# A graph-network layer on one core: 24 source columns a step on VectorE and on ScalarE, and six rows a step fetched by SyncE

## The chip, the core and the metric

The kernel runs on one core of a Trainium2 chip. The core has TensorE (PE in the profile; PEld is its weight loads), VectorE (DVE), ScalarE (ACT), GpSimd (POOL) and SyncE (SP), and 16 DMA engines that all of them share. Each engine works off its own list of instructions in order. An engine's list also holds instructions that its sequencer carries out itself (reading numbers into registers, computing an address, waiting for a semaphore, issuing a DMA); the profile does not count these as busy time of the engine.

The metric is the device time of one execution in microseconds (us), as the median of three runs. The profile is one further execution, with a time of its own.

## The reference

One layer of a graph network with residual and layer norm. There are 12,500 nodes of 64 features and 212,500 edges, sorted by the node they go to:

```python
msg_in = concat([nodes[row], nodes[col], edge_features], -1)
messages = relu(msg_in @ mW1 + mb1) @ mW2 + mb2
aggregated = segment_sum(messages, col, num_segments=12500)
upd_in = concat([nodes, aggregated], -1)
x = layernorm(x + relu(upd_in @ uW1 + ub1) @ uW2 + ub2)
```

`row` is the source of an edge and random; `col` is its destination, and rises along the list. All of it is in 32-bit floats.

## The kernel before

**Groups and steps.** The edges are cut into 554 groups of 384 (three tiles of 128). The loop in lines 718 to 777 makes one step for each group. In step `k` TensorE does three things one behind the other, with a single wait ahead of them and a single signal after the last (`step`, line 677): it transposes the gathered sources of group `k` (`turn`, line 423), multiplies group `k-2` by the message weights (`hidden`, line 448), and sums group `k-4` over destinations (`sums`, line 474). When the step has ended, ScalarE copies the transposed sources out of PSUM (line 440) and applies ReLU (line 464), and VectorE adds the sums into the aggregate (line 495) and the counts (line 496). TensorE's next step does not wait for these; the one after it does. The last ten groups (`SHORT`) take the three parts in a different order.

**Where the sources come from.** A group's 384 source rows reach the chip in one of two ways. Most groups are gathered by GpSimd: `gather` (line 181) issues one indirect DMA for each tile of 128 rows, 16 groups ahead (`AHEAD`), into a ring of 20 buffers. Every tenth or eleventh group is "columned" (`COPIED`): all nodes lie transposed in SBUF in `own.xc`, and VectorE and ScalarE copy one column of 64 floats for each edge from there to the group's place in `own.st` (`fetch`, line 585). Such a group needs no gather. `COLS` columns are copied in a step; `VCOLS` and `ACOLS` say how many by which engine and in which parts. Before, VectorE copies 12 and then 8 in a step, and ScalarE 16.

**Registers.** A column's address is read from a list in SBUF into a register. `registers(k, part)` (line 565) reads the addresses of one part with one instruction, TENSOR_LOAD (line 578), which the engine's sequencer carries out. `fetch(part)` then hands out that part's copies. Before, VectorE's part of 12 is loaded ahead of the additions (the list `between`, lines 493 and 738), its part of 8 just ahead of its copies, and ScalarE's part of 16 at the end of the step before (line 771). A further TENSOR_LOAD on VectorE, every fourth step, reads four registers that place the sums (`places`, line 366).

**SyncE.** For each step it issues the load of a 32-row window of projected nodes (`window`, line 390), every fourth step a block of edge features (`inputs`, line 355) into one of `BLOCKS` buffers, and every eighth step a list of column addresses (`indexes`, line 552). A window waits for TensorE to be done with the buffer.

**An unused path.** `STREAMS` describes single rows that an engine's queue can fetch by plain DMAs: the last tile of some groups (`BY_ROWS`) is then filled row by row (`row_numbers`, `row_fetch`, lines 632 and 652) into a buffer `own_side`, and not gathered. Before, the list is empty.

The destinations rise, so finished nodes can be updated while later groups are still worked on: every 22 steps or so `update` (line 500) runs the second network and the layer norm over 512 nodes, in pieces spread over several steps.

Of the kernel before, what the change touches and what calls it, by code (L numbers as in the profile page):

```python
# [32 lines left out]
G = (E + GE - 1) // GE  # L33
SB = 4
AHEAD = 16
RING = AHEAD + 4
BLOCKS = 4
NW = 2 * SB
COUNT = 96
NH = 3  # L40
# [9 lines left out]
TIMES = 4  # L50
BEGIN = 18
CHECKED = 8
VCOLS = (12, 8)
ACOLS = (16,)
COLS = sum(VCOLS + ACOLS)
SPAN = 8
STREAMS = ()
ROW_TURNS = 8
ROW_LEAD = 3

# [1 line left out]
def tiles_of(g):  # L62

    n = min(GE, E - g * GE)
    return [min(P, n - j * P) for j in range((n + P - 1) // P)]
# [26 lines left out]
BY_ROWS = []  # L92
for _, rate, _ in STREAMS:
    BY_ROWS.append([])
    while True:
        last = BEGIN + (P * (len(BY_ROWS[-1]) + 1) - 1) // rate + ROW_LEAD
# [7 lines left out]
class Own:  # L104
# [4 lines left out]
    def __init__(self, nc, ctx):  # L109
        def on(name, *shape, of=nc.sbuf_tensor):  # L110
            return ctx.enter_context(of(name, list(shape), F32)).ap()

        self.s = [on(f"own_s{i}", P, TG, D + W) for i in range(RING)]
        self.st = [on(f"own_st{i}", P, SB * GE) for i in range(BLOCKS)]
        self.wm = [on(f"own_wm{i}", P, H) for i in range(NW)]
        self.h = [on(f"own_h{i}", P, TG, H) for i in range(NH)]
        self.side = [[on(f"own_side{n}{i}", P, D + W) for i in range(2)]
                     for n in range(len(STREAMS))]
        self.ident = on("own_ident", P, P)
# [10 lines left out]
def ordered(ctx: ExitStack, tc: tile.TileContext, a, own, ok):  # L130
# [28 lines left out]
    def after(first, *others):  # L159

        tc.declare_no_dep(first.ins, group="quiet", reason="waits for the last of a step")
        for i in others:
            tc.add_manual_dep(
                first.ins, i.ins.name,
                mybir.DependencyInfo(mybir.DependencyClass.Sync, mybir.DependencyReason.DATA),
                reason="the kernel's own rings",
            )
        return first
# [73 lines left out]
    def bit(k):  # L242

        nodes = [NEAR_NODES + (N - NEAR_NODES) * i // BITS for i in (k, k + 1)]
        tiles = [first + (NT - first) * i // BITS for i in (k, k + 1)]
        nc.sync.dma_start(src_sb[:, slice(*tiles)], a["src"][:, slice(*tiles)])
        nc.sync.dma_start(xc[:D, slice(*nodes)], a["xT"][:, slice(*nodes)])
        rest(nodes[0], nodes[1] if k < BITS - 1 else NP)

    def zeroed(k):  # L250

        n0, n1 = (NP * i // BITS for i in (k, k + 1))
        nc.vector.memset(agg[:, n0:n1], 0.0)
# [58 lines left out]
    rows_by, row_index = {}, {}  # L312
    fetched = [[] for _ in STREAMS]
    issuers = {"SP": (nc.sync, ET.SP), "PE": (nc.tensor, ET.PE)}
# [40 lines left out]
    def inputs(b):  # L355
        if b * SB >= G:
            return
        c0, c1 = b * SB * GE, min(E, (b + 1) * SB * GE)
        efs_by[b] = nc.sync.dma_start(own.st[b % BLOCKS][D + W :, : c1 - c0], a["efT"][:, c0:c1])
        after(efs_by[b], *([hidden_by[(b - BLOCKS + 1) * SB - 1]] if b >= BLOCKS else []))  # L360

    def columns(g):
        t, c = own.st[g // SB % BLOCKS], (g % SB) * GE
        return t, c, sum(tiles_of(g))
# [58 lines left out]
    def turn(g, ps):  # L423
# [11 lines left out]
        def copy(step):  # L435
# [4 lines left out]
                after(nc.scalar.activation(t[r, c : c + n], xt[r, :n], AF.Copy), step))]  # L440
            if g >= BLOCKS * SB:
                after(copies[0], hidden_by[g - BLOCKS * SB])
            copy_by[g] = copies
# [30 lines left out]
    def sums(g, ps):  # L474
        h, s = own.h[g % NH], own.s[g % RING]
        sizes = tiles_of(g)
        sg = ps[2][:, : TIMES * W].rearrange("p (t w) -> p t w", w=W)
        counted = ps[2][0:1, TIMES * W :][:, :W]
        did = []
        for j, p in enumerate(sizes):  # L480
            did.append(nc.tensor.matmul(  # L481
                sg, h[:p, j, :],
                s[:p, j, D:].unsqueeze(1).to_broadcast([p, TIMES, W]),
                start=j == 0, stop=j == len(sizes) - 1))
        for j, p in enumerate(sizes):
            did.append(nc.tensor.matmul(counted, own.one[:p], s[:p, j, D:],  # L486
                                        start=j == 0, stop=j == len(sizes) - 1))

        def add(step):
            sums_by[g] = step  # L490
            at = bass.ds(starts.pop(g), W)
            count = xc[COUNT : COUNT + 1, at]
            if between:
                between.pop()()
            a = after(nc.vector.tensor_tensor(agg[:, at], sg[:, 0, :], agg[:, at], ALU.add), step)  # L495
            return [a, after(nc.vector.tensor_tensor(count, counted, count, ALU.add), step)]  # L496

        return did, [*relu_by[g], *copy_by[g]], add
# [66 lines left out]
    def registers(k, *parts):  # L565

        i, n = divmod(k - BEGIN, SPAN)
        if i < 0:
            return
        all_parts = [*((ET.DVE, c) for c in VCOLS), *((ET.Activation, c) for c in ACOLS)]  # L570
        for part in parts:
            engine, count = all_parts[part]
            c0 = (k - BEGIN) * COLS + sum(c for _, c in all_parts[:part])
            count = min(count, GE * len(COPIED) - c0)
            if count <= 0:
                return
            b = c0 - i * SPAN * COLS
            _, v = nc.values_load_multi_w_load_instructions(
                indices[i][0:1, b : b + count], engines=[engine],
                min_val=own.at, max_val=own.at + 4 * (N - 1),  # L580
                skip_runtime_bounds_check_because="a source is one of the nodes",
            )
            held[part] = engine, c0, v
# [28 lines left out]
    def row_span(n, i):  # L612

        _, rate, steps = STREAMS[n]
        size = ROW_TURNS * rate * steps
# [16 lines left out]
    def row_numbers(n, k):  # L632

        _, rate, steps = STREAMS[n]
        q, r = divmod(k - BEGIN, steps)
# [4 lines left out]
        if some > 0:  # L640
            _, v = nc.values_load_multi_w_load_instructions(
                row_index[n, i][0:1, b : b + some], engines=[issuers[STREAMS[n][0]][1]],
                min_val=0, max_val=4 * D * (N - 1),
# [69 lines left out]
    for n in range(len(STREAMS)):  # L713
        row_indexes(n, 0)
    made = summed = 0
    between, held, last = [], {}, {}

    for k in range(G):
        if k < BITS:
            bit(k)  # L720
            if k + 2 < BITS:
                zeroed(k + 2)
        if 1 < k < len(TABLE):
            projected(k)
        if k == CHECKED:
            addresses(0)
            for n in range(len(STREAMS)):
                row_addresses(n, 0)
            combined()
            ordered_edges()  # L730
            early.close()
            up = ctx.enter_context(tc.tile_pool(name="upd", bufs=2))
        if k % SB == 2:
            inputs(k // SB + 2)
        if k % SB == 1:
            places(k // SB + 1)
        if k < G - SHORT:
            between.append(lambda: registers(k, 0))
            step((turn, k), *([(hidden, k - 2)] if k > 1 else []),
                 *([(sums, k - 4)] if k > 3 else []))  # L740
            made, summed = max(0, k - 1), max(0, k - 3)
            if between:
                between.pop()()
        else:

            step((turn, k))
            for _ in range(2):
                if summed < made:
                    step((sums, summed))
                    summed += 1  # L750
            for _ in range(2):
                if made <= k:
                    step((hidden, made))
                    made += 1
            registers(k, 0)
        fetch(0)
        window(k + SB)
        for n in range(len(STREAMS)):
            row_numbers(n, k)
            row_fetch(n)  # L760
        onehot(k + LEAD)
        marks_by[k] = [copy_by[k][-1]]
        if k < G - 1:
            for part in range(1, len(VCOLS + ACOLS)):
                if part != len(VCOLS):
                    registers(k, part)
                fetch(part)
                if part >= len(VCOLS) and ET.Activation in last:
                    marks_by[k].append(last[ET.Activation])
            if k + 1 < G - 1:  # L770
                registers(k + 1, len(VCOLS))
            if k >= BEGIN and (k - BEGIN) % SPAN == 0:
                indexes((k - BEGIN) // SPAN + 1)
            if k >= BEGIN and (k - BEGIN) % SPAN == SPAN - 2:
                addresses((k - BEGIN) // SPAN + 1)
        if k + AHEAD < G:
            gather(k + AHEAD)
# [333 lines left out]
```

## Time and profile before

| what | value |
|---|---|
| median of three runs | 1914.63 us (1913.1 to 1914.86) |
| the profiled execution's own time | 1914.16 us |
| its span, first to last instruction | 1912.4 us |
| granted TensorE clock, mean | 0.972 |
| indirect gathers on POOL | 1514 |
| column copies on DVE and ACT | 10460 and 8356 |
| busy share of the span: POOL, PE, ACT, DVE | 75%, 69%, 69%, 65% |

A group row of the page names the line, the engine, the operation and the tiles, then the count, the busy time in us, the mean duration of one in ns, and the idle time of the engine just ahead of these instructions with what ended it. In a timeline row the first number is the start in us, the second how long the merged instructions took, and a bracket gives the idle time ahead and its releaser. "DVEq" and "ACTq" are those engines' sequencers, and a row of theirs gives the shortest, median and longest duration in ns.

### The profile page before, as it was taken

The page shows a single profiled execution, that of the slowest core. Times are in us where ns is not written, and L with a number is a line of the kernel's source. Part 1 is how long each engine was busy: PE and PEld are TensorE (multiplying, and loading weights), DVE is VectorE, ACT ScalarE, POOL GpSimd, SP SyncE. Part 2 cuts the span into 40 slices and gives each one's busy share as a digit, 9 for nine tenths or more (in the row PEclk, how much of TensorE's full clock was granted, in tenths as well). Part 3 has the DMA queues.
Part 4 walks back from the last instruction along what each step waited for, and adds up shares of the span by engine and source line. Part 5 has one row for each costly group of instructions (what it writes and reads, how often), then busy time and mean ns, then how long its engine had stood idle before and what let it go on. Part 6 is the DMA issues. An engine that isn't in the chain of part 4 may idle for free. (4 is left out here: it accounts for less than half of the span.)

```text
span 1912.4 us, 56586 instructions
## 1 busy us (share of the span) xinstructions
PE 1324.3 (69%) x12323; PEld 1170.6 (61%) x12323; DVE 1251.4 (65%) x12584; ACT 1325.2 (69%) x9559; POOL 1431.7 (75%) x1521
## 2 busy tenths in 40 slices
PE   5877777767767766676666776766766766667677
PEld 4766666666656655665655665655656655556566
DVE  4347777766666666676766766666667666676662
ACT  4468787766767767776767776776676677676662
POOL 7777777777777777777777777777777777777774
PEclk9889999989999999999999999999999999999998
DMA  5532222222222222222222212222222222222221
GB/s 141 139 97 64 53 50 52 49 49 48 45 53 52 46 52 48 49 49 48 53 48 48 50 44 53 52 46 52 48 50 48 51 47 52 45 53 48 49 50 25
DMA packets 113836, 105.15 MB, mean 55 GB/s; under 512 B 52115, under 2 KB 83488, under 8 KB 113488
## 3 DMA queue, kind: packets, MB, share of 16 engines
q0 software_dynamic: 48448, 49.68, 13.6%
q1 hardware_dynamic: 64196, 51.29, 9.7%
q8 instruction: 104, 1.70, 0.4%
q14 instruction: 244, 2.00, 0.3%
q10 hardware_dynamic: 844, 0.48, 0.1%
HBM read 91.68 MB, written 9.62 MB: 53 GB/s over the span
## 5 line engine op out<-in xcount | busy, mean ns | idle before, releaser
L184 POOL DMA_INDIRECT own_s<-in_x,src_sb x1514 | 1430.9, 945 | 462.5 <-issue 261.5
L599 DVE COPY own_st<-own_xc 64x4 uint8 x10460 | 896.5, 191 | 27.7 <-DMA by_dst<-t 3.5
L601 ACT ACTIVATE own_st<-own_xc 64x4 uint8 x8356 | 847.3, 195 | 2.9 <-DMA by_dst<-t 2.9
L429 PE MATMUL own_ps<-own_ident,own_s 128*96 128x128 f32 x1661 | 289.0, 284 | 540.4 <-DMA own_s<-in_x,src_sb 355.6
L440 ACT ACTIVATE own_st<-own_ps 96x384 f32<-96x384 f32 (+1 forms) x554 | 268.6, 485 | 506.7 <-PE own_ps L486 483.7
L429 PEld LDWEIGHTS own_ps<-own_ident,own_s 128*96 128x96 f32 x1661 | 164.3, 129 | 602.0 <-ACT own_h L464 445.0
L481 PE MATMUL own_ps<-own_s,own_h 128*128 128x128 f32 x3322 | 478.6, 282 | 1.3 <-ACT own_h L464 0.6
L495 DVE TENSOR_TENSOR own_agg<-own_ps,own_agg 128x32 f32 x554 | 106.3, 192 | 567.1 <-PE own_ps L486 386.4
L453 PE MATMUL own_ps<-own_wm,own_st 128*128 128x128 f32 x3322 | 476.5, 281 | 0.0
L481 PEld LDWEIGHTS own_ps<-own_s,own_h 128*128 128x128 f32 x3322 | 431.1, 198 | 2.8 <-ACT own_h L464 1.6
L453 PEld LDWEIGHTS own_ps<-own_wm,own_st 128*128 128x128 f32 x3322 | 428.6, 197 | 1.3 <-issue 0.5
L464 ACT ACTIVATE own_h<-own_ps 128x384 f32<-128x384 f32 x553 | 264.8, 479 | 21.2 <-PE own_ps L453 20.0
L486 PE MATMUL own_ps<-own_s,own_one 128*1 128x32 f32 x3322 | 189.1, 194 | 0.0
L486 PEld LDWEIGHTS own_ps<-own_s,own_one 128*1 128x1 f32 x3322 | 113.8, 83 | 69.4 <-issue 5.7
L412 DVE TENSOR_TENSOR own_s<-iota,dlc 128x96 f32<-128x96 f32 x554 | 137.3, 248 | 0.7
L496 DVE TENSOR_TENSOR own_xc<-own_ps,own_xc 1x32 f32 x554 | 102.1, 184 | 31.9 <-PE u_ps L507 13.2
L383 PE MATMUL u_ps<-w1b,own_xc 65*128 65x128 f32 x196 | 31.8, 310 | 32.0 <-DMA own_xc<-in_xT 12.7
L383 PEld LDWEIGHTS u_ps<-w1b,own_xc 65*128 65x128 f32 x196 | 26.8, 211 | 35.0 <-issue 20.3
L519 PE MATMUL u_ps<-same,own_xc 65*128 65x64 f32 (+1 forms) x196 | 39.5, 283 | 0.4 <-ACT u L512 0.4
L386 ACT ACTIVATE t<-u_ps 128x512 f32<-128x512 f32 (+1 forms) x25 | 14.7, 588 | 36.2 <-DMA by_dst<-t 20.0
L521 PE MATMUL u_ps<-u,u 128*128 128x64 f32 (+1 forms) x196 | 38.2, 277 | 0.0
L519 PEld LDWEIGHTS u_ps<-same,own_xc 65*128 65x128 f32 (+1 forms) x196 | 29.9, 192 | 2.5 <-ACT u L512 1.0
(60 smaller groups left out, 264.4 us busy)
## 6 DMA issues: line engine op xcount, KB each, us to landing
own_st<-in_efT SPq DMA_DIRECT2D x138, 192.0 KB
own_s<-in_x,src_sb POOLq DMA_INDIRECT x1514
own_wm<-by_dst SPq DMA_DIRECT2D x554, 16.0 KB
by_dst<-t SPq DMA_DIRECT2D x24, 256.0 KB
out<-o SPq DMA_DIRECT2D x24, 128.0 KB
own_xc<-in_xT SPq DMA_DIRECT2D x12, 179.2 KB
index<-in_src_copied SPq DMA_DIRECT2D x65, 1.1 KB
dlc_i<-in_dst_cols SPq DMA_DIRECT2D x1, 807.0 KB
```

The costliest lines, as they stand in the source:

```text
L184: nc.gpsimd.indirect_dma_start(out=s[:p, j, :D], out_offset=None, in_=x[:, :], in_offset=bass.IndirectOffsetOnAxis(ap=src_sb[:p, g * TG + ...
L412: places_by[g] = nc.vector.tensor_tensor(own.s[g % RING][:, :, D:], iota.unsqueeze(1).to_broadcast([P, TG, W]), dlc[:, g * TG : (g + 1) * ...
L429: nc.tensor.transpose(xt[:, j * P : j * P + p], sides[g] if g in sides and j == TG - 1 else s[:p, j, :], ident[:p, :p])
L440: after(nc.scalar.activation(t[r, c : c + n], xt[r, :n], AF.Copy), step))]
L453: nc.tensor.matmul(pre[:p, j, :], t[:, c + j * P : c + j * P + p], wm[g % NW], start=True, stop=True)
L464: relu_by[g] = [nc.scalar.activation(h, pre, AF.Relu)]
L481: did.append(nc.tensor.matmul(sg, h[:p, j, :], s[:p, j, D:].unsqueeze(1).to_broadcast([p, TIMES, W]), start=j == 0, stop=j == len(sizes) - 1))
L486: did.append(nc.tensor.matmul(counted, own.one[:p], s[:p, j, D:], start=j == 0, stop=j == len(sizes) - 1))
L495: a = after(nc.vector.tensor_tensor(agg[:, at], sg[:, 0, :], agg[:, at], ALU.add), step)
L496: return [a, after(nc.vector.tensor_tensor(count, counted, count, ALU.add), step)]
L599: by[engine] = nc.vector.tensor_copy(o, x_at)
L601: by[engine] = nc.scalar.activation(o, x_at, AF.Copy)
```

## The change

The constants change, and so do the places where registers are loaded.

```diff
-BLOCKS = 4
+BLOCKS = 3
-VCOLS = (12, 8)
-ACOLS = (16,)
+VCOLS = (12, 4, 4, 4)
+ACOLS = (12, 4, 4, 4)
-STREAMS = ()
+STREAMS = (("SP", 6, 2),)
...
         def add(step):
...
-            if between:
-                between.pop()()
             a = after(nc.vector.tensor_tensor(agg[:, at], sg[:, 0, :], agg[:, at], ALU.add), step)
...
         if k < G - SHORT:
-            between.append(lambda: registers(k, 0))
             step((turn, k), *([(hidden, k - 2)] if k > 1 else []),
                  *([(sums, k - 4)] if k > 3 else []))
...
-            if between:
-                between.pop()()
         else:
...
-            registers(k, 0)
+        registers(k, 0)
+        if k < G - 1:
+            registers(k, len(VCOLS))
         fetch(0)
...
                 if part >= len(VCOLS) and ET.Activation in last:
                     marks_by[k].append(last[ET.Activation])
-            if k + 1 < G - 1:
-                registers(k + 1, len(VCOLS))
```

With 48 columns a step, 65 groups are columned, where it was 49. With six rows a step, read into registers twelve at a time every second step, 24 tiles are filled by rows. Together these leave 1442 of the 1514 gathers. Line numbers above 57 are lower in the changed kernel: the additions stand in lines 493 and 494, the register loads in 576, the copies in 597 (VectorE) and 599 (ScalarE).

On VectorE, one step of the middle of the program before, from the addition (L495, L496) to the end of the step; L412 builds the one-hot of a later group:

```order
L495 TENSOR_TENSOR own_agg<-own_ps,own_agg 128x32
L496 ISA
L496 TENSOR_TENSOR own_xc<-own_ps,own_xc 1x32
L599 COPY own_st<-own_xc 64x4 x12
L412 TENSOR_TENSOR own_s<-iota,dlc 128x3x32
L578 TENSOR_LOAD index
L599 COPY own_st<-own_xc 64x4 x8
L578 TENSOR_LOAD index
```

The same step of VectorE in the changed kernel:

```order
L493 TENSOR_TENSOR own_agg<-own_ps,own_agg 128x32
L494 ISA
L494 TENSOR_TENSOR own_xc<-own_ps,own_xc 1x32
L576 TENSOR_LOAD index
L597 COPY own_st<-own_xc 64x4 x12
L412 TENSOR_TENSOR own_s<-iota,dlc 128x3x32
L576 TENSOR_LOAD index
L597 COPY own_st<-own_xc 64x4 x4
L576 TENSOR_LOAD index
L597 COPY own_st<-own_xc 64x4 x4
L576 TENSOR_LOAD index
L597 COPY own_st<-own_xc 64x4 x4
```

The load of 12 has moved from ahead of the addition to behind it; one load of 8 has become three of 4, each ahead of its four copies.

On ScalarE, a step before (L440 copies the transposed sources, L464 is the ReLU):

```order
L440 ACTIVATE own_st<-own_ps 96x384
L464 ACTIVATE own_h<-own_ps 128x384
L601 ACTIVATE own_st<-own_xc 64x4 x16
L578 TENSOR_LOAD index
```

The same step of ScalarE in the changed kernel, up to its second part:

```order
L440 ACTIVATE own_st<-own_ps 96x384
L464 ACTIVATE own_h<-own_ps 128x384
L576 TENSOR_LOAD index
L599 ACTIVATE own_st<-own_xc 64x4 x12
L576 TENSOR_LOAD index
L599 ACTIVATE own_st<-own_xc 64x4 x4
```

The load that stood at the step's end now stands between the ReLU and the first copies, and two more pairs of a load and four copies follow.

On SyncE, four steps of the middle of the program before (L402 is the window, L359 the edge features, L396 reads four registers):

```order
L396 TENSOR_LOAD start_b
L402 DMA own_wm<-by_dst 32x512 x2
L359 DMA own_st<-in_efT 32x1536
L402 DMA own_wm<-by_dst 32x512 x2
```

About two and a half steps of SyncE in the changed kernel (L639 reads twelve registers, L654 fetches rows):

```order
L396 TENSOR_LOAD start_b
L402 DMA own_wm<-by_dst 32x512
L639 TENSOR_LOAD row_index_48572
L654 DMA own_side<-in_x 1x256 x6
L402 DMA own_wm<-by_dst 32x512
L654 DMA own_side<-in_x 1x256 x6
L359 DMA own_st<-in_efT 32x1536
L402 DMA own_wm<-by_dst 32x512
```

Six row fetches stand behind every window, and a load of twelve registers ahead of every second six.

More of the change, by code (lines that the diff above doesn't have):

```diff
@@ L715, in ordered @@
     made = summed = 0
-    between, held, last = [], {}, {}
+    held, last = {}, {}
     for k in range(G):
```

## The prediction, made before the changed kernel ran

> **What bounds the kernel now.** I read the page's list of engines and the costliest groups first, then the stretch in which columns are copied, then single steps.
>
> ```profile
> span 1912.4 us, 56586 instructions
> PE 1324.3 (69%) x12323; PEld 1170.6 (61%) x12323; DVE 1251.4 (65%) x12584; ACT 1325.2 (69%) x9559; POOL 1431.7 (75%) x1521
> L184 POOL DMA_INDIRECT own_s<-in_x,src_sb x1514 | 1430.9, 945 | 462.5 <-issue 261.5 <-DMA own_s<-in_x,src_sb 173.7 <-ACT own_h L464 10.7
> L495 DVE TENSOR_TENSOR own_agg<-own_ps,own_agg 128x32 f32 x554 | 106.3, 192 | 567.1 <-PE own_ps L486 386.4 <-DVE own_st L599 77.4 <-PE u_ps L506 47.3
> ```
>
> No engine is busy for more than 75%, yet POOL is full: its 1514 gathers take 1430.9 us and leave 462.5 us between them, 1.251 us for each gather, and 1514 of those are 1893 of the span's 1912.4 us. The 0.3 us ahead of a gather is named after several releasers but is always about the same, so it belongs to the gather. POOL is the bound, and the addition on DVE mostly waits for PE, which waits for gathers.
>
> The stretch in which columns are copied, by the first and the last addition in it and by two tables of instructions:
>
> ```profile
> 95.15 0.19 DVE L495 TENSOR_TENSOR own_agg<-own_ps,own_agg 128x32 f32 x1 [5.99 <-PE own_ps L486]
> 1855.23 0.19 DVE L495 TENSOR_TENSOR own_agg<-own_ps,own_agg 128x32 f32 x1 [1.41 <-PE own_ps L486]
> 95.20:1855.30 1760.10, 100.18 (x523) 0.98 0.23 51
> 95.20:1855.30 1760.10, 1330.42 (x1410) 0.98 0.23 51
> ```
>
> The third row counts additions, 523: 522 steps in 1760.1 us, 3.372 us a step. The fourth counts gathers, 1410, one in 1.248 us.
>
> The question is how near the other engines are to 3.372 us. For DVE I looked for steps in which nothing outside holds it: the addition's wait is ended by DVE's own copies.
>
> ```profile
> 1471.56 0.19 DVE L495 TENSOR_TENSOR own_agg<-own_ps,own_agg 128x32 f32 x1 [0.55 <-DVE own_st L599]
> 1471.78 0.18 DVE L496 TENSOR_TENSOR own_xc<-own_ps,own_xc 1x32 f32 x1
> 1471.99 1.02 DVE L599 COPY own_st<-own_xc 64x4 uint8 x12
> 1472.87 0.24 DVE L412 TENSOR_TENSOR own_s<-iota,dlc 128x96 f32<-128x96 f32 x1
> 1473.04 0.67 DVE L599 COPY own_st<-own_xc 64x4 uint8 x8
> 1474.25 0.19 DVE L495 TENSOR_TENSOR own_agg<-own_ps,own_agg 128x32 f32 x1 [0.54 <-DVE own_st L599]
> ...
> 1150.21 0.19 DVE L495 TENSOR_TENSOR own_agg<-own_ps,own_agg 128x32 f32 x1 [1.01 <-DVE own_st L599]
> 1153.34 0.19 DVE L495 TENSOR_TENSOR own_agg<-own_ps,own_agg 128x32 f32 x1 [0.97 <-DVE own_st L599]
> ```
>
> The first step lasts 2.70 us from addition to addition, the second 3.13 us. In both, half a microsecond to one is idle although DVE's last copy is long over. The register loads account for it:
>
> ```profile
> L578 DVEq TENSOR_LOAD <-index x1046: 592/844/1106, 88.7 to 1855.9; - x175
> L578 ACTq TENSOR_LOAD <-index x523: 313/1021/1340, 90.2 to 1852.7; - x175
> L371 DVEq TENSOR_LOAD <-start_i x139: 340/343/812, 10.5 to 1882.2; - x139
> L371 DVEq TENSOR_LOAD <-start_i x1: 347/347/347, 1151.8 to 1151.8; - x1
> L578 DVEq TENSOR_LOAD <-index x1: 594/594/594, 1472.2 to 1472.2; - x1
> L578 DVEq TENSOR_LOAD <-index x1: 846/846/846, 1473.1 to 1473.1; - x1
> ```
>
> On DVE a load of 12 registers takes 0.846 us (the last row), one of 8 takes 0.594 us, and one of 4 takes 0.343 us (L371); on ACT one of 16 takes 1.021 us. The sequencer does them in its order, next to nothing else: in the first step above the load of 8 runs from 1472.2 while the copies go on, and that of 12 from 1473.1, and the next addition can only be handed out when it is over. The second step also holds an L371 load (the row at 1151.8). So **DVE has a floor of 2.70 us a step, set by its sequencer and not by its busy time**, and a load of 4 lengthens it by 0.43 us.
>
> **The change, part by part.** *Gathers.* 1514 less 1442 is 72 gathers of 1.251 us: 90 us less on POOL, whose own end would come at 1822 us of span.
>
> *DVE's loads and copies.* From 2.70 us I take away the load of 8 with what surrounds it (0.594 and 0.09, the difference between 0.43 and 0.343): 0.68. I add three loads of 4: 3 x 0.43 = 1.29. Four more copies must be handed out. Between 1472.2 + 0.594 and 1473.1 the sequencer hands out eight, some 0.3 us, 0.04 each; four are 0.15 (bounds: 0, and 4 x 0.07 from twelve copies in 0.94 to 1.02 us). The load of 12 is there as before; it moves behind the additions, where it no longer overlaps the wait for PE, but in a step that DVE itself sets there is no such wait. The floor becomes 2.70 - 0.68 + 1.29 + 0.15 = **3.46 us**, above the present mean step already.
>
> The Trainium skill, "Perfetto Trace Analysis", section "Sequencer-only Instruction (DRAIN, etc)", says that the profile reports only the execution of such an instruction, and that what comes before and after is a hidden tail. By durations alone the floor would be 2.70 - 0.59 + 1.03 + 0.15 = 3.29 us, some 88 us less over 520 steps; the trace agrees with the page, since two steps that differ by one load of 0.343 us differ by 0.43.
>
> *What else DVE does.* L371 comes every fourth step: 0.43 / 4 = 0.11 us. The node updates and the address lists:
>
> ```profile
> L543 DVE TENSOR_SCALAR o<-u_ps,mv,rstd 128x64 f32<-128x64 f32 (+1 forms) x98 | 27.0, 337 | 1.0
> L563 DVE TENSOR_SCALAR index<-index 1x288 int32<-1x288 int32 x66 | 22.2, 336 | 0.1
> L528 DVE BATCH_NORM_STATS2 stats<-u_ps 128x6 f32<-128x64 f32 (+1 forms) x98 | 20.4, 208 | 5.3 <-PE u_ps L521 5.3
> L529 DVE BATCH_NORM_AGGREGATE mv<-stats 128x2 f32<-128x6 f32 (+1 forms) x98 | 17.8, 182 | 3.5
> L540 DVE RECIPROCAL rstd<-rstd 128x4 f32<-128x4 f32 (+1 forms) x25 | 4.4, 176 | 0.4 <-ACT rstd L535 0.4
> ```
>
> They sum to 91.8 us, 0.18 us a step (lower bound 0.10, where the sequencer runs ahead under them). Last, the addition waits for a semaphore of DVE's own. If that tells of the last copies, which now end later than the sequencer's last load, up to 0.13 us is added (a copy's 0.16 to 0.19 us less the time to set up the addition); the other bound is nothing, as in the steps above. I take 0.05. The mean step is 3.46 + 0.11 + 0.18 + 0.05 = **3.80 us**, bounds 3.65 and 4.0.
>
> *ACT.* A step that ACT itself sets:
>
> ```profile
> 853.80 0.49 ACT L440 ACTIVATE own_st<-own_ps 96x384 f32<-96x384 f32 x1 [3.94 <-PE own_ps L486]
> 854.19 0.48 ACT L464 ACTIVATE own_h<-own_ps 128x384 f32<-128x384 f32 x1
> 854.56 1.62 ACT L601 ACTIVATE own_st<-own_xc 64x4 uint8 x16
> 856.16 0.49 ACT L440 ACTIVATE own_st<-own_ps 96x384 f32<-96x384 f32 x1
> ```
>
> It lasts 2.36 us. Eight more copies at 0.095 (1.62 us for 16, less the last one's tail) make 3.12. The load of 12, about 0.78 between the 313 and 1021 ns of 4 and 16, now runs between ReLU and copies; it can start when ReLU is handed out and delays the copies by 0.2 to 0.4 us where it isn't hidden by the copy and ReLU ahead. The small loads hide behind twelve copies of 1.1 us. That is 3.1 to 3.5 us: below DVE's step, so its cover is DVE, and without that cover it would cost nothing against today's step either, or 0.1.
>
> *SyncE.* Six row DMAs a step, and half a load of 12.
>
> ```profile
> L402 SPq MOVE own_wm<-by_dst x554: 29/29/38, 13.8 to 1871.9; - x185
> L402 SPq DMA_DIRECT2D own_wm<-by_dst x554: 315/316/1247, 15.3 to 1872.2; - x185
> L402 SPq EVENT_SEMAPHORE  x544: 17/17/3006, 13.8 to 1871.9; - x182
> 1004.27 0.27 SPq L557 DMA_DIRECT2D index<-in_src_copied  x1
> 1004.70 4.25 SPq L402 DMA_DIRECT2D own_wm<-by_dst  x3
> SPq L402 <- PE own_ps L486: 780.6, 332, 5.9
> ```
>
> A row DMA isn't in this trace. The nearest is L557, one stretch of one row: 0.27 us; the upper bound is the window with its 32 rows, 0.316. Each also has an address to move (0.029) and gaps: from 1004.54 to 1004.70 there are three gaps beside 0.046 of work, 0.04 each. That is 0.38 to 0.47 for one (the upper end with a semaphore instruction of its own), 2.3 to 2.8 for six. With 0.45 for half a load of 12, 0.47 for the window and 0.3 for the rest SP needs 3.5 to 4.0 us a step. I take 3.55, by L557. It is hidden behind DVE, and SP waited 780.6 us for PE before. `BLOCKS = 3` makes the edge features wait for step k-1 rather than k-5; they are needed eight steps later: nothing.
>
> *Sum.* 520 steps copy columns (24,960 columns, 48 a step). 520 x (3.80 - 3.372) = 223 us. After the last copies 57 us of the span are left, fourteen steps of up to three gathers; POOL will be ahead there, so 5 us come off. 1912.4 + 223 - 5 = 2130 us of span. The profiled execution took 1914.16, 1.8 more than its span and within 0.5 of the median, so I forecast **2132 us**, DVE's sequencer as the bound in place of POOL.
>
> **The rivals.** *SyncE becomes the bound.* If a row costs what a window costs, six take 2.8 and the step 4.0 us or more: 1912 + 520 x 0.63 = 2240 us, and up to 2290 with loads like L578's longest. For it: the two estimates overlap. Against: L557's 0.27.
>
> *POOL stays the bound.* If the sequencer's small loads ran beside the copies at no cost, DVE would need its busy time only: 24 copies at 0.07, a one-hot and two additions, some 2.4 us. The step is then set by gathers, 1442 x 1.251 plus the 19 us that are not POOL's: 1823 us, **faster** by 91. The point from which it decides is a DVE step of 1442/1514 of today's, 3.2 us. Against it stands the 0.43 us between the two kinds of step.
>
> *About even.* The loads of 4 cost only 0.30 each and the updates hide: 3.07 + 0.11 + 0.10 and slow copies, near 3.37: 1915 us. No row speaks for it.
>
> **How the numbers follow.** DVE's sequencer 0.80; SyncE 0.13; POOL 0.04; about even 0.03. The forecast's own bounds, 3.65 and 4.0 us, give 520 x 0.28 = 146 and 520 x 0.63 = 328: 2055 to 2240; its upper end lies far out (all bounds at once), so I let the range end at 2235 with most of SyncE's case in it. Runs of this kernel lie within 0.2% of each other, so 0.2% is what can be told from no change: slower 0.94, faster 0.04, same 0.02.
>
> **What would show it.** DVE's additions come 3.8 us apart, and 3.4 to 3.5 in steps without other work; the wait ahead of the additions names DVE's own copies, and no longer PE, in most steps. Register loads of 4 read about 343 ns on DVE. Gaps ahead of gathers grow beyond 0.3 us, named after ACT or DVE, since the ring is full. ACT waits for PE in most steps. If instead PE waits for `own_side` or `own_wm`, SyncE is the bound; if POOL's gaps stay at 0.3 us, I was wrong about DVE.

## The result, and the profile after

| | us, median | lowest to highest | runs |
|---|---|---|---|
| before | 1913.99 | 1913.1 to 1914.86 | 4 |
| changed | 2077.41 | 2067.57 to 2087.14 | 4 |

The changed kernel takes 1.0854 of the time before (95% interval 1.0795 to 1.0912): 163 us more. Its profiled execution took 2082.68 us, with a span of 2080.9. In the experiments 5 to 12 below, the kernel of before itself took 2504 to 2543 us, at a granted clock of 0.80 to 0.83 where it was 0.96 to 0.98, so there only the ratio to that kernel on the same chip, and durations that are the same in both, are used.

The page of the changed kernel, its list of engines and four of its groups (behind the bar: busy time in all, mean ns of one, then idle time ahead and who ended it):

```profile
span 2080.9 us, 72072 instructions
PE 1381.2 (66%) x12323; PEld 1219.9 (59%) x12323; DVE 1447.2 (70%) x14659; ACT 1740.9 (84%) x13683; POOL 1363.7 (66%) x1449
L184 POOL DMA_INDIRECT own_s<-in_x,src_sb x1442 | 1363.0, 945 | 644.7 <-ACT own_st L440 213.9
L597 DVE COPY own_st<-own_xc 64x4 uint8 x12480 | 1115.0, 185 | 463.2 <-issue 436.8
L599 ACT ACTIVATE own_st<-own_xc 64x4 uint8 x12480 | 1250.7, 193 | 43.5 <-DVE own_xc L494 34.3
L493 DVE TENSOR_TENSOR own_agg<-own_ps,own_agg 128x32 f32 x554 | 106.7, 193 | 113.5 <-PE own_ps L486 69.4
```

POOL has 68 us less to do than before and yet stands idle 182 us longer. Much of that is now named after ACT: 213.9 us after its copy in L440, and in the list of waits 185.4 us after its column copies (L599). A name is not yet a cause; the experiments have to tell. DVE hardly waits for PE any more ahead of the addition (69.4 us, where it was 386.4). In its place 463.2 us are idle ahead of its own copies, where it was 27.7, and 436.8 of them are "issue": nothing that the profile shows held DVE back. It is 70% busy. PE has 57 us more to do than before, at a granted clock of 0.942 where it was 0.972; but ahead of its first matmul of a step (L429) it waits 627.4 us, and all but 56.5 of them name another engine or a DMA, so its clock is not what holds the steps.

The stretch in which columns are copied, by its first and last addition and by a table of additions (number in brackets):

```profile
96.50 0.19 DVE L493 TENSOR_TENSOR own_agg<-own_ps,own_agg 128x32 f32 x1 [6.68 <-PE own_ps L486]
2022.96 0.19 DVE L493 TENSOR_TENSOR own_agg<-own_ps,own_agg 128x32 f32 x1 [0.36 <-DVE own_st L597]
96.40:2026.20 1929.80, 100.21 (x520) 0.94 0.22 47
```

520 additions are 519 steps in 1926.5 us: **3.71 us a step**, where it was 3.372. One step in which DVE has nothing else to do, and the register loads of its sequencer in it (ns, then where they start):

```profile
1000.77 0.19 DVE L493 TENSOR_TENSOR own_agg<-own_ps,own_agg 128x32 f32 x1 [0.29 <-DVE own_st L597]
1001.00 0.18 DVE L494 TENSOR_TENSOR own_xc<-own_ps,own_xc 1x32 f32 x1
1001.91 0.94 DVE L597 COPY own_st<-own_xc 64x4 uint8 x12 [0.73 <-issue]
1002.77 0.24 DVE L412 TENSOR_TENSOR own_s<-iota,dlc 128x96 f32<-128x96 f32 x1
1002.94 1.29 DVE L597 COPY own_st<-own_xc 64x4 uint8 x12
1004.16 0.19 DVE L493 TENSOR_TENSOR own_agg<-own_ps,own_agg 128x32 f32 x1
...
L576 DVEq TENSOR_LOAD <-index x1: 847/847/847, 1001.0 to 1001.0; - x1
L576 DVEq TENSOR_LOAD <-index x1: 346/346/346, 1002.3 to 1002.3; - x1
L576 DVEq TENSOR_LOAD <-index x1: 342/342/342, 1002.9 to 1002.9; - x1
L576 DVEq TENSOR_LOAD <-index x1: 341/341/341, 1003.4 to 1003.4; - x1
```

The step lasts 3.39 us. From 1001.0 to 1001.85 the load of 12 runs and DVE stands idle 0.73 us behind its addition; that is the "issue" of the page. Then come three loads 0.5 to 0.6 us apart, each with four copies handed out behind it. 0.847 + 0.346 + 0.342 + 0.341 = 1.88 of the 3.39 us are register loads.

### The profile page after: what moved, and what is told of

The parts are those of the page before. It is cut to its first block, busy times and chain, and to the rows that moved or that the text cites. A ratio compares the mean times of both kernels' runs of the same rounds, so it can differ in the third digit from the quotient of the medians.

```text
span 2080.9 us, 72072 instructions
## 1 busy us (share of the span) xinstructions
PE 1381.2 (66%) x12323; PEld 1219.9 (59%) x12323; DVE 1447.2 (70%) x14659; ACT 1740.9 (84%) x13683; POOL 1363.7 (66%) x1449
## 5 line engine op out<-in xcount | busy, mean ns | idle before, releaser
L184 POOL DMA_INDIRECT own_s<-in_x,src_sb x1442 | 1363.0, 945 | 644.7 <-ACT own_st L440 213.9
L597 DVE COPY own_st<-own_xc 64x4 uint8 x12480 | 1115.0, 185 | 463.2 <-issue 436.8
L599 ACT ACTIVATE own_st<-own_xc 64x4 uint8 x12480 | 1250.7, 193 | 43.5 <-DVE own_xc L494 34.3
L429 PE MATMUL own_ps<-own_ident,own_s 128*96 128x128 f32 x1637 | 295.6, 291 | 627.4 <-ACT own_h L464 381.7
L429 PEld LDWEIGHTS own_ps<-own_ident,own_s 128*96 128x96 f32 x1637 | 167.7, 133 | 691.9 <-ACT own_h L464 410.9
L481 PE MATMUL own_ps<-own_s,own_h 128*128 128x128 f32 x3322 | 498.8, 290 | 2.8 <-ACT own_h L464 2.3
L453 PE MATMUL own_ps<-own_wm,own_st 128*128 128x128 f32 x3322 | 495.3, 289 | 0.0
L481 PEld LDWEIGHTS own_ps<-own_s,own_h 128*128 128x128 f32 x3322 | 451.0, 206 | 5.0 <-ACT own_h L464 3.9
L453 PEld LDWEIGHTS own_ps<-own_wm,own_st 128*128 128x128 f32 x3322 | 447.8, 205 | 1.7 <-issue 0.5
L440 ACT ACTIVATE own_st<-own_ps 96x384 f32<-96x384 f32 (+1 forms) x554 | 266.3, 481 | 179.2 <-PE own_ps L486 163.7
L464 ACT ACTIVATE own_h<-own_ps 128x384 f32<-128x384 f32 x553 | 264.7, 479 | 22.8 <-PE own_ps L453 21.2
L493 DVE TENSOR_TENSOR own_agg<-own_ps,own_agg 128x32 f32 x554 | 106.7, 193 | 113.5 <-PE own_ps L486 69.4
L412 DVE TENSOR_TENSOR own_s<-iota,dlc 128x96 f32<-128x96 f32 x554 | 136.3, 247 | 0.8
L533 ACT ACTIVATE rstd<-mv,eps 128x4 f32<-128x4 f32 (+1 forms) x25 | 7.4, 297 | 45.2 <-DVE mv L527 45.2
L504 PE MATMUL u_ps<-own_agg,wc 128*128 128x512 f32 (+1 forms) x50 | 28.1, 644 | 24.3 <-DVE own_agg L493 24.3
```

The lines of the kernel that those rows point to most:

```text
L184: nc.gpsimd.indirect_dma_start(out=s[:p, j, :D], out_offset=None, in_=x[:, :], in_offset=bass.IndirectOffsetOnAxis(ap=src_sb[:p, g * TG + ...
L412: places_by[g] = nc.vector.tensor_tensor(own.s[g % RING][:, :, D:], iota.unsqueeze(1).to_broadcast([P, TG, W]), dlc[:, g * TG : (g + 1) * ...
L429: nc.tensor.transpose(xt[:, j * P : j * P + p], sides[g] if g in sides and j == TG - 1 else s[:p, j, :], ident[:p, :p])
L453: nc.tensor.matmul(pre[:p, j, :], t[:, c + j * P : c + j * P + p], wm[g % NW], start=True, stop=True)
L464: relu_by[g] = [nc.scalar.activation(h, pre, AF.Relu)]
L481: did.append(nc.tensor.matmul(sg, h[:p, j, :], s[:p, j, D:].unsqueeze(1).to_broadcast([p, TIMES, W]), start=j == 0, stop=j == len(sizes) - 1))
```

## The experiments

My theory: DVE's sequencer is the bound, and what loads it is the *number* of register loads. Rivals: ACT's 24 columns, SyncE's rows, or the loads' new places behind the additions. Runs 1 to 4 ran on one chip, with the kernel before at 1913.6 us there (1912.95 to 1915.41, 8 runs).

### 1. Six loads of 4 on VectorE

```diff
-VCOLS = (12, 4, 4, 4)
+VCOLS = (4, 4, 4, 4, 4, 4)
```

> The changed kernel with VectorE's 24 columns in six parts of 4 (ScalarE, rows and the rest unchanged). VectorE's sequencer as the bound: the load of 12 with its copies and the one-hot (1.34 us in the changed kernel's trace) gives way to three loads of 4 with four copies each (0.547 us each, from the same trace) and the one-hot's hand-out (0.03): +0.33 us a step, plain steps of 3.72 us, 520 steps, about 2250 us. ScalarE or SyncE as the bound: VectorE's extra loads hide, 2077 us give or take 15.

Measured: 2249.65 us, 1.1753 of before (1.173 to 1.1777), 172 us more than the changed kernel. Its loads on DVE, a table of additions, and part of a step:

```profile
L576 DVEq TENSOR_LOAD <-index x3120: 335/340/684, 96.3 to 2195.4; - x195
200.00:1800.00 1600.00, 76.78 (x398) 0.89 0.20 42
1003.70 0.38 DVE L597 COPY own_st<-own_xc 64x4 uint8 x4
1004.24 0.38 DVE L597 COPY own_st<-own_xc 64x4 uint8 x4 [0.17 <-issue]
1004.78 0.39 DVE L597 COPY own_st<-own_xc 64x4 uint8 x4 [0.16 <-issue]
```

The same 24 columns, the same copies: only two loads a step more, and 398 steps in 1600 us, 4.02 us each. The pairs of a load and four copies follow each other at 0.54 us, 0.38 busy and 0.16 idle: a load of 0.34 us, and the hand-out of four copies and what surrounds the load in the other 0.2. Steps without other work (DVE does its additions, the copies and one one-hot, and no L371 load) have a median of 3.69 us in the trace, where the changed kernel has 3.39.

### 2. Two loads of 12 on VectorE

```diff
-VCOLS = (12, 4, 4, 4)
+VCOLS = (12, 12)
```

> The changed kernel with VectorE's 24 columns in two parts of 12 (ScalarE, rows and the rest unchanged). VectorE's sequencer as the bound: three pairs of a load of 4 and four copies (1.64 us) give way to one load of 12 and twelve copies (1.31 us): plain steps of 3.06 us for VectorE, 0.33 less, about 1905 us if nothing else takes over, up to 1940 where ScalarE (3.17 us in its steps that wait for nothing) or POOL (3.22 us by its gathers) takes over. ScalarE as a second bound at the present 3.7 us: 2040 us or more. SyncE as the bound: no change, 2070 us.

Measured: 1935.0 us (1920.75 to 1937.88, 5 runs), 1.0088 of before (1.0058 to 1.0118). **142 of the change's 163 us are gone** with two loads a step fewer, at the same 48 columns, rows and places. The engines, DVE's loads, the additions counted, two additions in a row, and four rows of ACT:

```profile
PE 1348.1 (70%) x12323; PEld 1191.8 (62%) x12323; DVE 1387.2 (72%) x14659; ACT 1706.1 (88%) x13683; POOL 1364.2 (70%) x1449
L576 DVEq TENSOR_LOAD <-index x1040: 842/848/1218, 96.6 to 1878.8; - x174
200.00:1800.00 1600.00, 87.83 (x471) 0.96 0.23 49
1003.44 0.17 DVE L493 TENSOR_TENSOR own_agg<-own_ps,own_agg 128x32 f32 x1
1006.48 0.18 DVE L493 TENSOR_TENSOR own_agg<-own_ps,own_agg 128x32 f32 x1
1004.04 0.47 ACT L440 ACTIVATE own_st<-own_ps 96x384 f32<-96x384 f32 x1
1004.41 0.47 ACT L464 ACTIVATE own_h<-own_ps 128x384 f32<-128x384 f32 x1
1004.78 2.38 ACT L599 ACTIVATE own_st<-own_xc 64x4 uint8 x24
1007.07 0.47 ACT L440 ACTIVATE own_st<-own_ps 96x384 f32<-96x384 f32 x1
```

ACT's work is untouched here, so ACT cannot have been what made a step last 3.71 us. A step is now 1600 / 471 = 3.40 us in the mean. In the rows above two engines fill the step: ACT works from end to end, 3.03 us from L440 to L440 with no idle time, and DVE's additions lie 3.04 us apart, with two loads of 0.85 us in each step. Which of the two sets the step now is open, and no run took work off one of them alone from here.

### 3. Two loads of 12 on ScalarE

```diff
-ACOLS = (12, 4, 4, 4)
+ACOLS = (12, 12)
```

> The changed kernel with ScalarE's 24 columns in two parts of 12 (VectorE, rows and the rest unchanged). VectorE's sequencer as the bound: no change beyond the spread of the changed kernel, 2065 to 2090 us. ScalarE as a bound (84% busy, and POOL and PE wait for it by name): two loads and their surroundings fewer, 0.1 to 0.3 us a step, 1920 to 2025 us.

Measured: 2077.67 us (2061.49 to 2088.11, 4 runs), 1.0859 of before (1.079 to 1.0928): no difference from the changed kernel's 1.0854 that can be told. The same edit that was worth 142 us on DVE is worth nothing on ACT. This says less on the bound than I had meant it to: in the changed kernel ACT is idle for only 43.5 us ahead of all its column copies, 34.3 of them waiting for DVE, so its loads were hidden already, and two fewer could hardly make it faster. From L440 to L440 its steps without idle time have a median of 3.15 us in both traces. That ACT isn't the bound rests on run 2. What run 3 shows is that a short load costs nothing on an engine whose copies cover it.

### 4. No rows

```diff
-STREAMS = (("SP", 6, 2),)
+STREAMS = ()
```

> The changed kernel without the row stream: 24 tiles more are gathered by POOL. VectorE's sequencer as the bound: no change but for the row addresses that VectorE no longer scales (0.1 us every sixteenth step, 3 us), since POOL has 197 us of waits beyond its fixed gaps and the 24 gathers need 30: 2060 to 2088 us. SyncE as the bound: six row DMAs of 0.32 us and half a load of 0.8 us fewer a step, 100 us faster or more.

Measured: 2062.33 us (2056.97 to 2074.89, 4 runs), 1.0797 of before (1.0758 to 1.0835), with 24 gathers more. The median is 15 us below the changed kernel's and the intervals overlap, so whether the rows cost some 0.7% stays open. That SyncE is the bound, with 100 us or more on it, is out.

### 5 and 9. The loads in their old places

The kernel of before, with all of the change but the places of the loads; run twice, on different chips.

```diff
-BLOCKS = 4
+BLOCKS = 3
-VCOLS = (12, 8)
-ACOLS = (16,)
-STREAMS = ()
+VCOLS = (12, 4, 4, 4)
+ACOLS = (12, 4, 4, 4)
+STREAMS = (("SP", 6, 2),)
```

> The kernel before with the four constants of the change (48 columns a step in parts of 12, 4, 4, 4, rows by SyncE, three buffers) but with the loads where they were: VectorE's load of 12 ahead of the additions, ScalarE's at the end of the step before. The number of loads as the cause: VectorE's sequencer has the same work in another order, 2.70 - 0.94 + 1.64 = 3.40 us in plain steps, so no change from the changed kernel, 2060 to 2095 us. The place of the loads as the cause: 2000 us or less, towards the 1840 us that 1442 gathers leave.

> Once more the kernel before with the four constants of the change and its loads where they were (VectorE's 12 ahead of the additions, ScalarE's at the step's end), since the chip of the second call took 2541 us for the kernel before. The number of loads as the cause: 3.40 us in VectorE's plain steps, no change from the changed kernel, 2060 to 2095 us where the kernel before takes 1914. The place as the cause: 2000 us or less.

Measured: 2601.07 against 2541.29, 1.0219 (1.0175 to 1.0263); and 2600.6 against 2540.73, 1.0221 (1.0188 to 1.0254). The times that were expected belong to 1914 us for the kernel before and can't be held against these.

### 6. The old columns, with the loads in their new places

```diff
-VCOLS = (12, 4, 4, 4)
-ACOLS = (12, 4, 4, 4)
-STREAMS = (("SP", 6, 2),)
+VCOLS = (12, 8)
+ACOLS = (16,)
+STREAMS = ()
```

`BLOCKS` is 4 again too.

> The changed kernel with the old constants (12 and 8 columns on VectorE, 16 on ScalarE, no rows, four buffers): only the places of the loads differ from the kernel before. The number of loads as the cause: VectorE's floor stays at 2.70 us, POOL stays the bound with 1514 gathers, 1910 to 1920 us. The place as the cause: a load of 0.85 us stands behind the addition in every step in which VectorE has waited for TensorE, 1950 us or more.

Measured: 2568.48 against 2541.29, 1.0101 (1.0059 to 1.0143). That lies between the two expectations, no change and 1.9% or more.

### 12. The changed kernel again

Unchanged, so that it can be held against run 9.

> The changed kernel itself, to set beside the kernel with the same constants and the loads in their old places (2600.6 us on the chip that takes 2541 us for the kernel before). The number of loads as the cause: the two are alike, 2580 to 2620 us there, and plain steps of VectorE with a floor of 3.39 us in both. The place of the loads as the cause: 2650 us or more. On a chip that takes 1914 us for the kernel before: 2060 to 2090 us, the spread seen so far.

Measured: 2543.24 against 2503.68, 1.0157 (1.013 to 1.0184). Its loads on VectorE are as long as in the first profile, where the median is 345 ns too:

```profile
L576 DVEq TENSOR_LOAD <-index x2080: 339/345/1103, 169.9 to 2486.8; - x190
```

I had expected this run and run 9 to be alike. The change costs 1.6% here with the loads in the new places and 2.2% with them in the old ones, on different chips, and the intervals just fail to meet; at the old columns the new places cost 1.0%. So at 48 columns the new places are, if anything, the better. The shortest steps without other work (the fifth in a hundred, of those with all their loads inside) last 3.39 us in run 9, with four loads in the old places, and 3.34 in run 12 (3.35 in the changed kernel's first profile); in the kernel before the same reading gives 2.70, with two loads. The lengthening comes with the loads in either place. What the old places would be worth where the kernel before takes 1914 us was not measured; there, run 2 has the new places and only 0.9% of the 8.5% left. Why the same change costs 1.6% here and 8.5% there is not shown.

### 7 and 8. 22 columns on VectorE, 24 on ScalarE

The kernel of before with two loads on each engine; run 8 also fetches four rows a step on SyncE, with `BLOCKS = 3`.

```diff
-VCOLS = (12, 8)
-ACOLS = (16,)
+VCOLS = (12, 10)
+ACOLS = (12, 12)
```

> The kernel before with 12 and 10 columns on VectorE and 12 and 12 on ScalarE, loads where they were, no rows. If each engine's own step is what the traces say, VectorE needs 2.70 + 2 x 0.094 = 2.89 us in plain steps and 3.2 in the mean, ScalarE about 3.1, and POOL with 1475 gathers of 1.251 us stays the bound: 1475 x 1.251 + 19 = 1864 us, up to 1885 where bursts of VectorE's longer steps show. If a load more on ScalarE costs its step as much as on VectorE (0.43 us): still below POOL's. If columns are dearer than this: 1914 us or more.

> The same with four rows a step by SyncE and three buffers. 1459 gathers: 1844 us if POOL stays the bound, up to 1870 where VectorE (3.2 us in the mean, against 3.26 for POOL's gathers in a step) holds some steps. SyncE needs about 3.27 us a step in the changed kernel with six rows, so 2.6 with four: no bound. If the rows cost what they save: 1864 us or more.

Measured: 2885.42 against 2541.29, 1.1361 (1.1308 to 1.1415); and 2892.04, 1.1367 (1.1306 to 1.1428). The loads of run 7 (lowest, median, highest ns), and a step of it on DVE:

```profile
L578 DVEq TENSOR_LOAD <-index x1036: 849/1842/3094, 172.4 to 2818.8; - x173
L578 ACTq TENSOR_LOAD <-index x1035: 313/2592/3229, 172.2 to 2812.1; - x173
...
1004.73 0.96 DVE L599 COPY own_st<-own_xc 64x4 uint8 x12
1005.61 0.24 DVE L412 TENSOR_TENSOR own_s<-iota,dlc 128x96 f32<-128x96 f32 x1
1007.64 0.80 DVE L599 COPY own_st<-own_xc 64x4 uint8 x10 [1.79 <-issue]
```

DVE stands still for 1.79 us between its copies. Half of DVE's loads, 518 of 1036, take more than 2 us: those of every second step, 2.74 us for the 12 and 2.30 for the 10, in between 0.85 and 1.08. On ACT it is the other half of the steps, 2.6 us against 0.79. A step has 46 columns, so DVE's loads begin at column 0 and 12, then at 46 and 58, and ACT's at 22 and 34, then at 68 and 80. All that begin at a multiple of four are short, and all others long. The load of 10 is dear even then, 1.08 us where 12 take 0.85. The runs were meant to show a better split and showed this instead; they say nothing on the theory.

### 10 and 11. 20 columns on VectorE, 24 on ScalarE, four rows

44 columns, so that all loads begin at a multiple of four and hold a multiple of four; one kernel, run twice.

```diff
-BLOCKS = 4
+BLOCKS = 3
-ACOLS = (16,)
+ACOLS = (12, 12)
-STREAMS = ()
+STREAMS = (("SP", 4, 2),)
```

> The kernel before with VectorE's 12 and 8 columns as they are, ScalarE's 24 in 12 and 12, four rows a step by SyncE and three buffers; loads where they were, and every part begins at a multiple of four registers. 60 columned groups and 16 tiles by rows leave 1465 gathers: 1465 x 1.251 + 19 = 1852 us if POOL stays the bound. VectorE's floor is unchanged (2.70 us, 3.0 in the mean), ScalarE needs 2.36 + 8 x 0.095 + 0.1 = 3.2 us, SyncE 2.6, all below POOL's 3.27. Up to 1880 if ScalarE's second load costs 0.2 us more. 1914 or more if a load costs ScalarE's step what it costs VectorE's and the steps are bursty.

> Once more the kernel before with 12 and 8 columns on VectorE, 12 and 12 on ScalarE, four rows a step and three buffers, where the kernel before takes 1914 us: 1465 gathers of 1.251 us and 19 us, 1852 us if POOL stays the bound, up to 1880 if ScalarE's second load costs its step 0.2 us more. 1914 us or more if a second load on ScalarE costs the step 0.4 us and ScalarE takes over. On a chip that takes 2541 us for the kernel before: no word on either.

Measured: 2549.63 against 2540.73, 1.0043 (1.0025 to 1.006); and 2552.15 against 2543.35, 1.0043 (1.0021 to 1.0064). The loads of run 10:

```profile
L578 DVEq TENSOR_LOAD <-index x1048: 592/843/1175, 171.1 to 2497.0; - x175
L578 ACTq TENSOR_LOAD <-index x1047: 545/782/1157, 170.6 to 2496.3; - x175
```

No median load is above 0.85 us now, which bears out the reading of run 7. The gain that I expected did not come. It was worked out for 1914 us of the kernel before, and whether 44 columns beat that kernel there stays open; no version that ran beat it.

## Why the prediction was right, point by point

**The bound.** It was right that POOL's bound gives way to DVE's sequencer. Runs 1 and 2 show it from both sides, with ACT and SyncE untouched: two loads more on DVE cost 172 us, and two fewer give back 142. The waits alone would not have told it, since those of PE and POOL are named after ACT. For each load more, at the same 24 columns, a step without other work is 0.15 us longer (3.69 less 3.39, halved).

**The floor** was sized at 3.46 us; the median of the 304 steps of the changed kernel without other work is 3.39. By durations alone it would have been 3.29, so part of the time around each load is real, and not all of the 0.09 that I put on each. The rows that carry it: a pair of a load of 4 and four copies takes 0.54 to 0.55, where I had put 0.43 and up to 0.15. Steps with an L371 load are 0.42 us longer than those without, as before. The Trainium skill's remark on a hidden tail behind such instructions ("Perfetto Trace Analysis", "Sequencer-only Instruction (DRAIN, etc)") agrees with this trace: 0.08 us beside the 0.344 of the load itself have no row in the trace.

**The rest of the step.** L371 is 0.42 / 4 = 0.105 (0.11 was said). The mean over those 304 steps is 3.47, 0.09 above their median, since about 80 of them are 0.35 us longer; that term I did not have. The updates are what remains of the mean of 3.71: some 0.13, where I had 0.18. The 0.05 for the addition's own wait can't be told from the floor: the list of waits has 20.2 us of it in 60 steps, and it lies within the 3.39. The two together were put at 3.51.

**The sum.** 3.80 was forecast, 3.71 measured. 520 steps by 0.088 are 46 us of the 49 by which the span of 2080.9 lies below the forecast 2130. The term that was mis-sized is the floor with the addition's own wait, 0.12 too much; the updates were 0.05 too much, and the 0.09 of longer steps was missing. That this last error makes up for half of the others is luck. The tail is the rest: 520 x (3.712 - 3.372) = 177 us, the span grew by 168.5, so 8 us came off outside these steps, where I had 5.

**ACT** was to need 3.1 to 3.5 us behind DVE. In the changed kernel it is hidden, since run 2 is 142 us faster with the same work on ACT. In the rows of run 2, with the same loads, it takes 3.03 from end to end, a little less than the lower end: the load of 12 hides wholly behind L440 and ReLU. What I had said of the case without cover, that it costs nothing against today's step or 0.1, is near what run 2 gives, 3.40 us a step and 1.0088, though DVE's own 3.04 us stand beside ACT's there.

**SyncE** was to need 3.5 to 4.0. The rows of L654 in the changed kernel, one fetch of a row with its address, and SyncE's waits for DVE and for PE:

```profile
L654 SPq MOVE own_side<-in_x x3072: 29/29/38, 116.5 to 1990.7; - x192
L654 SPq DMA_DIRECT2D own_side<-in_x x3072: 224/228/351, 116.6 to 1990.7; - x192
SPq L546 <- DVE own_xc L494: 175.8, 22, 16.4
SPq L402 <- PE own_ps L486: 9.8, 17, 3.3
```

A row takes 0.228 + 0.029, not 0.27 + 0.029. SyncE still waits for DVE, 175.8 us in one line, and without its rows run 4 is 15 us faster by the medians, not 100. Its room has shrunk all the same: its windows wait 9.8 us for PE, where they waited 780.6 before. The rival had rested on a row costing what a window costs (0.315); it does not.

**What I said would show it.** Of these, four held: additions 3.4 us apart in bare steps, loads of 4 at about 343 ns, longer gaps ahead of gathers named after ACT, and hardly a wait of PE for rows (9.2 us in all). Two did not. The wait ahead of the additions names DVE's own copies only seldom, and is short in all; what is idle stands ahead of the copies as "issue", because the long load now lies there. And ACT waits for PE less than I thought, 163.7 us in 175 waits, a third of the steps.

## What to carry to other kernels

An engine at 70% can be the bound: add up what its sequencer does between two of its instructions, register loads above all, and compare that with the step, not the busy share. Where values are read into registers on the engine that sets the step, few long loads beat many short ones, since each load has a price of its own (here 0.15 us of step, beside 0.063 for a register). Whether the short ones hide behind the copies that they feed depends on the copies: on VectorE four copies last 0.38 us, but their load and hand-out take 0.54 of the one sequencer that does both; on ScalarE, whose 24 copies last 2.38 us, the loads were hidden. And before a split is tried, see that each part begins at a multiple of four and holds a multiple of four.

## What the runs showed of the hardware

**Register loads.** On DVE 4 registers take 0.34 us, 8 take 0.59 and 12 take 0.85 (from the rows above and those before). From 8 to 12 and from 4 to 8 it is 0.25 each, 0.063 a register; the rest, 0.09, is for the load, and up to 0.08 more stands around it. A load that does not begin at a multiple of four took 2.3 to 2.7 us (run 7). Both 2.74 for 12 and 2.30 for 10 are 0.23 a register, and the 1.08 of a load of 10 that begins at one is the 0.59 of 8 and twice 0.24. That is as if whole fours were read together and all else one by one; no run tried it, and the trace does not show why.

**Longer steps now and then.** The 0.35 us in about every fourth bare step are gaps between hand-outs with no wait that the profile shows. The page's queue of instructions moved more than before, in packets of 8 KB:

```profile
q14 instruction: 367, 3.00, 0.5%
```

Before it was 244 packets with 2.00 MB: 123 more packets for 15486 more instructions, 126 for each packet. In the trace, 65 of the 78 longer bare steps hold the start of such a packet, and 78 of 207 others do. The two go together, then, but by its count the queue brings the instructions of all engines, and 13 of the longer steps hold no packet; that the gaps are waits for such packets is argued, and no run tried it.
